# The second last image's last projection and routing, moved beside the last image's first mixture

## The chip, the cores and the metric

The kernel runs on one core of a Trainium2 chip. TensorE (PE), VectorE (DVE), ScalarE (ACT) and GpSimd (POOL) each work through their own instruction stream in order; SyncE (SP) issues the DMAs in order too. The time is device microseconds for one execution; the median of several executions is given. Beside it stands one execution taken with the hardware profiler, from which all durations come.

## The reference

Four images of 32 x 32 positions and 256 channels pass through four layers, each image on its own. A token is one position, so an image is 1024 tokens.

```python
# layer 0: convolution and a selective scan over 512 channels with 64 states
x = layernorm(src) @ w_in + b_in;  x = gelu(depthwise_conv3x3(x) + conv_b)
dt, Bm, Cm = split(x @ w_x);  dt = softplus(dt @ w_dt + dt_bias)
h = exp(dt * A) * h + (dt * x) * Bm          # for each token, in order
y = (h * Cm).sum(states) + x * D_skip
x = src + layernorm(y) @ w_out + b_out
# layer 1: grouped 3x3 bottleneck with a residual
# layer 2: masked attention with 8 heads, then a mixture of 8 experts (hidden 256), top 2
t = t + layernorm(ln(t) + attn(ln(t)));  t = t + moe2(ln(t))
# layer 3: selective scan over 512 channels with 16 states, then a mixture (hidden 512), top 2
p, gate = split(ln(t) @ W_in);  u = silu(p @ W_conv + b_conv)
B, C = split(u @ W_bc);  dt = softplus(u @ W_dt + b_dt)
h = exp(dt * A) * h + dt * B * u;  y = (h * C).sum(states) * silu(gate)
t = t + y @ W_out + b_out
t = t + moe3(ln(t))     # logits, softmax, two best experts, sum of weight * (gelu(x W1 + b1) W2 + b2)
```

## The kernel before

**The scans set the pace.** `SCANS` (line 31) lists eight scans as (layer, image), the last two being (3, 2) and (3, 3). `scans` (line 366) cuts each into units of 128 rows (channels times states) by 1024 tokens: 256 units for a layer 0 scan, 64 for a layer 3 scan, sixteen of them for each of four channel groups `d`. For unit k, `load` fetches dt, repeated over the states, into a `dA` tile (five buffers) by DMA; `decay` turns it to exp(dt * A) on ACT; `first` repeats dt * x over the states with two bf16 matmuls into `ps_rep` (two buffers, from the tile `S`); DVE multiplies this by B and runs the scan into `h`; POOL multiplies `h` by C; `pair` sums two units over the states on PE into `ps_y`, which ACT copies out and SP stores. B and C lie repeated over the partitions in the tiles `rows0` and `rows1`, two buffers each, fetched by `chunk` with `S`, `AHEAD` = 12 units ahead.

**All else is laid between the units.** Each stage of an image is a generator that issues some instructions and yields: `front` (layer 0 up to its scan), `middle` (line 1870: `back0`, `layer1`, `attention`, `moe(2)`, `front3`) and `last` (line 1880: `back3`, `moe(3)`, store of the image). `run` (line 562) steps through the scan units, adds up an estimate of each engine's time, and after each half unit calls `advance` (line 540) up to `TICKS` = 2 times while no other engine's sum is ahead of DVE's. Stages follow one another; the next is the first in `STAGES` whose scan is far enough. This is all decided when the program is built. On the chip each engine only follows its stream and its semaphores.

**Where a scan needs a stage.** A scan of layer 3 needs what `front3` writes for its image (`parts` and `dt`, for each `d`). `chunks_ahead` (line 414) looks for it 12 units ahead and puts it off while more than `LATEST` = 5 units remain. Then `need` (line 527) advances the stage until the data are written, with no scan unit between; `self.alone` tells the attention that it may use the scan's PSUM. For the last scan (3, 3), this comes five units before the end of scan (3, 2): the rest of image 3's attention, its `moe(2)` and `front3` up to its first channel group are issued there, and the last four units of scan (3, 2) are replicated, multiplied and scanned behind them.

**`back3` (line 1797)** fetches the tokens `t` kept by `front3`, and for each `d` the silu gate and y; a `Wait` holds it until that scan has stored y. POOL adds the bias row to the tokens (`add_rows`) and multiplies y by the gate (`gated`); PE projects with `W_out` into `ps_o`; DVE adds that to the tokens `tb`. **`moe` (line 1518)** fetches the first expert's weights; takes the norm (statistics on DVE, a log and an exponential on ACT, then the tokens through ACT); transposes on PE (`ps_tr`); multiplies by the router (`ps_lg`); finds the two best experts in `route` on DVE with one `Exp` on ACT; transposes the weights (`ps_ct`) and adds the experts' second bias (`ps_b`). Then it runs over 8 experts and two halves of the tokens: `one` issues the matmuls of `ps_h` and, one block later, `ps_e`; `two` issues `Gelu` on ACT and the weighted addition to `tb` on DVE. Weights have two buffers and are fetched one expert ahead. PSUM tiles of side work come from `ps` (line 180), three in rotation.

All pools of side work lie on the right side of SBUF, stacked. Where a helper records the call, the profile has line 124 for it.

Of the kernel before, what the change touches and what calls it, by code (L numbers as in the profile page):

```python
# [7 lines left out]
F32 = mybir.dt.float32  # L8
# [8 lines left out]
P = 128  # L17
NB = 4
# [23 lines left out]
AHEAD = 12  # L42
LATEST = 5


# [82 lines left out]

class Wait(tuple):
    pass  # L130


class Hybrid:
# [232 lines left out]
    def scans(self, mp, psum):  # L366
# [9 lines left out]
        for scan in SCANS:  # L376
            G = P // self.states[scan[0]]
            units += [
                (scan, d, c, i, j)
                for d in range(DC) for c in range(2) for i in range(32 // G) for j in range(2)  # L380
            ]
        chunks, rows, waiting = {}, {}, []
        state = {}
        self.scan_psum = psum
        y = None

        def chunk(k):

            if k >= len(units):
                return  # L390
            scan, d, c, i, j = units[k]
            if (c, i, j) != (0, 0, 0):
                return
            n = self.states[scan[0]]
            self.need(scan, d)
            if d == 0:
                bct = self.mem["bc", *scan]
                pair = []
                for t in range(2):
                    x = mp.tile([P, L], F32, tag=f"rows{t}", name=f"rows{t}", bufs=2)  # L400
                    nc.sync.dma_start(
                        x, bct[t * n : (t + 1) * n, :].unsqueeze(1).to_broadcast([n, P // n, L])
                    )
                    pair.append(x)
                rows[scan] = pair
            S = mp.tile([3 * 32, 4, L], BF16, tag="S", name="S", bufs=2)
            for s in range(3):
                nc.sync.dma_start(
                    S[32 * s : 32 * s + 32, :, :],
                    self.mem["parts", *scan, d][s].rearrange("(j p) t -> p j t", p=32),  # L410
                )
            chunks[scan, d] = S

        def chunks_ahead(k, late=False):

            if not late and k + AHEAD < len(units) and units[k + AHEAD][2:] == (0, 0, 0):
                waiting.append(k + AHEAD)
            while waiting:  # L420
                scan, d = units[waiting[0]][:2]
                if ("parts", *scan, d) not in self.ready:
                    if waiting[0] - k > LATEST:
                        break
                    if not late:
                        return True
                    self.alone = True
                chunk(waiting.pop(0))
                self.alone = False
            return False  # L430

        def load(k):
            if k >= len(units):
                return
            scan, d, c, i, j = units[k]
# [9 lines left out]
        def decay(k):  # L445
            if k >= len(units):
                return
            scan, d, c, i, j = units[k]
# [6 lines left out]
        def first(k):  # L455
            if k >= len(units):
                return
# [39 lines left out]
        for k in range(AHEAD):  # L497
            chunk(k)
        for k in range(4):
            load(k)  # L500
        decay(0)
        decay(1)
        first(0)
        for k in range(len(units) + 4):
            waits = chunks_ahead(k)
            load(k + 4)
            if not waits:
                first(k + 1)
            decay(k + 2)
            if k < len(units):  # L510
                a, inp = state.pop(k)
                B, Cm = rows[units[k][0]]
                nc.vector.tensor_tensor(inp, inp, B, ALU.mult)
            yield
            if k < len(units):
                h = mp.tile([P, L], F32, tag="h", name="h", bufs=5)
                nc.vector.tensor_tensor_scan(h, a, inp, 0.0, ALU.mult, ALU.add)
                nc.gpsimd.tensor_tensor(h, h, Cm, ALU.mult)
                state[k] = h
            if k % 2 == 1 and 2 <= k < len(units) + 2:  # L520
                pair(k - 2)
            if waits:
                chunks_ahead(k, True)
                first(k + 1)
            yield
# [991 lines left out]

    def moe(self, which, b, tb):

# [5 lines left out]
        KH = hidden // P  # L1525
        with tc.tile_pool(name=f"m{which}{b}", bufs=1, side="right") as op:
            xT = op.tile([P, 2, L], F32, name="xTm")
            cw = op.tile([P, TB, NEXP], F32, name="cw")

# [6 lines left out]

            weights = {0: expert_weights(0)}
            with tc.tile_pool(name=f"mg{which}{b}", bufs=1, side="right") as gp:
                xn = gp.tile([P, TB, C], F32, name="xnm")
# [51 lines left out]
                yield from self.pipe(range(TB // 2), last, add, cost=1.0)  # L1591

            hidden_of = {}
            got = {}
# [201 lines left out]

    def back3(self, b, tb):
        nc, tc = self.nc, self.tc
        with tc.tile_pool(name=f"h{b}", bufs=1, side="right") as sp:
            nc.sync.dma_start(tb, self.mem["t", b])  # L1800
# [69 lines left out]
    def middle(self, b):  # L1870

        with self.tc.tile_pool(name=f"t{b}", bufs=1, side="right") as tp:
# [3 lines left out]
            yield from self.attention(b, tb)  # L1876
            yield from self.moe(2, b, tb)
            yield from self.front3(b, tb)

    def last(self, b):  # L1880
        with self.tc.tile_pool(name=f"e{b}", bufs=1, side="right") as tp:
            tb = tp.tile([P, TB, C], F32, name="tb")
# [48 lines left out]
```

## Time and profile before

| | us |
|---|---|
| median of 3 executions | 6504.83 |
| lowest, highest | 6499.96, 6507.34 |
| profiled execution, its own time | 6499.29 |
| its span | 6497.3 |
| PE busy | 5253.9 (81%) |
| DVE busy | 5119.6 (79%) |
| ACT busy | 3415.4 (53%) |
| POOL busy | 3646.8 (56%) |

All times inside the kernel are counted from the start of the span. The page gives busy times, the span in 40 slices of 162 us, and groups of instructions as output tile<-input tiles, shapes and count. In a table of windows each row has the window, its length, busy us and number of instructions of PE, PE's weight loads, DVE, ACT and POOL, the granted PE clock as a share of full speed, the DMA engines' share and GB/s. One f32 matmul of the program appears as two records.

### The profile page before, as it was taken

To read this page: it belongs to the slowest core of one execution; us is meant where nothing else is said; L and a number is where in the kernel's file an instruction comes from. 1 tells how busy PE (TensorE), PEld (TensorE's weight loads), DVE (VectorE), ACT (ScalarE), POOL (GpSimd) and SP (SyncE) were. 2 spreads that over 40 slices of the span, in tenths; PEclk is the share of its full clock that TensorE was granted. 3 is DMA by queue.
4 is the path that set the end of the run, shared out by engine and by line. 5 is a ranking of instruction groups with operands and counts; after the bars stand their busy time and mean duration, and the time that the engine had idled before them with its cause. 6 is when DMAs were issued, how large, how long until landed. Compare 5 with 4: busy or idle time off the path is not lost. (4 is left out here: it accounts for less than half of the span.)

```text
span 6497.3 us, 59722 instructions
## 1 busy us (share of the span) xinstructions
PE 5253.9 (81%) x20235; PEld 2124.1 (33%) x20320; DVE 5119.6 (79%) x4310; ACT 3415.4 (53%) x4095; POOL 3646.8 (56%) x1793
## 2 busy tenths in 40 slices
PE   6667868689797569979689679798699688978979
PEld 2022212222342022234145232252255222524656
DVE  3978988988898998889889988898899981258311
ACT  3346656355576335567568445577387354246311
POOL 2957677765557666555856665556756661055200
PEclk9577868689898569979789789898699689878989
DMA  2454554643355566335635664345544750156221
GB/s 101 145 163 159 180 163 160 198 150 124 119 174 170 180 169 164 113 128 184 195 132 176 195 159 135 112 146 178 182 164 163 196 148 15 46 147 166 68 67 34
DMA packets 348077, 936.58 MB, mean 144 GB/s; under 512 B 37140, under 2 KB 119648, under 8 KB 346144
## 3 DMA queue, kind: packets, MB, share of 16 engines
q1 hardware_dynamic: 345616, 930.35, 46.0%
q0 software_dynamic: 2128, 2.13, 0.2%
q8 instruction: 168, 2.75, 0.2%
q14 instruction: 165, 1.35, 0.1%
HBM read 842.59 MB, written 93.95 MB: 144 GB/s over the span
## 5 line engine op out<-in xcount | busy, mean ns | idle before, releaser
L124 POOL TENSOR_TENSOR h<-h,rows 128x1024 f32<-128x1024 f32 x1280 | 3033.0, 2372 | 1835.8 <-DVE h L124 1572.9
L124 DVE TENSOR_TENSOR_SCAN h<-dA,ps_rep 128x1024 f32<-128x1024 f32 x1280 | 2923.7, 2284 | 131.4 <-ACT dA L124 3.1
L124 DVE TENSOR_TENSOR ps_rep<-ps_rep,rows 128x1024 f32<-128x1024 f32 x1280 | 1551.7, 1212 | 188.5 <-PE ps_rep L124 183.9
L124 ACT ACTIVATE dA<-dA,A_L_conv_A_log 128x1024 f32<-128x1024 f32 x1024 | 1147.7, 1144 | 612.1 <-DMA dA<-dt 547.2
L124 PE MATMUL ps_rep<-S,spread_L_conv_A_log 96*128 96x512 bf16 x2048 | 763.2, 463 | 767.6 <-DVE h L124 716.2
L124 PE MATMUL ps_y<-h,collect_L_conv_A_log 128*32 128x512 f32 x4096 | 775.8, 767 | 61.5 <-POOL h L124 61.0
L124 PE MATMUL ps_h<-xTm,we 128*128 128x512 f32 x1536 | 714.2, 604 | 0.0
L124 PE MATMUL ps_e<-we,h_m 128*128 128x256 f32 x3072 | 700.4, 380 | 2.3 <-ACT h_m L124 2.3
L124 PEld LDWEIGHTS <-spread_L_conv_A_log 96*128 96x128 bf16 x2048 | 159.9, 103 | 1568.9 <-DVE h L124 1236.1
L124 ACT ACT_TABLE_LOAD x483 | 619.7, 1283 | 59.4 <-PE ps_h L124 44.1
L124 PEld LDWEIGHTS ps_e<-we,h_m 128*128 128x128 f32 x3072 | 579.4, 190 | 152.5 <-issue 61.1
L124 DVE SCALAR_TENSOR_TENSOR tb<-ps_e,cw,tb 128x256 f32<-128x256 f32 x512 | 219.9, 474 | 409.3 <-PE ps_e L124 409.2
L124 ACT ACTIVATE h_m<-ps_h,cols 128x512 f32<-128x512 f32 x384 | 260.2, 687 | 501.4 <-PE ps_h L124 498.9
L124 ACT ACTIVATE p<-ps_sc 128x512 f32<-128x512 f32 x432 | 234.5, 594 | 386.0 <-PE ps_sc L124 255.4
L124 PEld LDWEIGHTS ps_h<-xTm,we 128*128 128x128 f32 x1536 | 291.9, 193 | 331.7 <-issue 286.9
L124 ACT ACTIVATE dA<-dA,A_L_attn_A_log 128x1024 f32<-128x1024 f32 x256 | 290.6, 1146 | 200.0 <-DMA dA<-dt 172.3
L124 PE MATMUL ps_rep<-S,spread_L_attn_A_log 96*128 96x512 bf16 x512 | 185.8, 451 | 173.8 <-DVE h L124 161.0
L124 PE MATMUL ps_at<-p,v 128*32 128x512 f32 x1024 | 277.6, 623 | 4.8 <-ACT sums L124 4.6
L124 PE MATMUL ps_at<-p,ones 128*32 128x512 f32 x1024 | 277.6, 623 | 0.0
L124 PE MATMUL ps_sc<-qT,kT 32*128 32x512 f32 x864 | 262.9, 665 | 14.2 <-ACTq L1318 8.1
L124 PE MATMUL ps_cv<-pad,diag 128*128 128x512 f32 x576 | 262.3, 597 | 0.0
L124 PEld LDWEIGHTS ps_y<-h,collect_L_conv_A_log 128*32 128x32 f32 x4096 | 99.4, 119 | 436.9 <-issue 222.6
(327 smaller groups left out, 4865.4 us busy)
## 6 DMA issues: line engine op xcount, KB each, us to landing
dA<-dt SPq DMA_DIRECT2D x1280, 512.0 KB
we<-in_L_ffn_W_dram SPq DMA_DIRECT2D x64, 512.0 KB
parts<-parts SPq DMA_DIRECT2D x64, 384.0 KB
S<-parts SPq DMA_DIRECT2D x96, 256.0 KB
dt<-sp_r SPq DMA_DIRECT2D x64, 256.0 KB
y<-yo SPq DMA_DIRECT2D x128, 128.0 KB
y_back<-y SPq DMA_DIRECT2D x64, 256.0 KB
we<-in_L_ffn_w_dram SPq DMA_DIRECT2D x64, 256.0 KB
```

Source lines behind the costliest of these rows:

```text
L124: return got(*args, **kw)
```

## The change

Five things are done.

- `DRAIN` = 4 empty entries stand in the list of units ahead of the first unit of the last scan, and that unit's data are waited for only one entry ahead (`LATEST` stays 5 for the others). So all 64 units of scan (3, 2) are issued, and their sums stored, ahead of the wait. `upto` issues `load` and `decay` for a unit only when its chunk has been fetched.
- B and C of a scan lie in one tile `rows`, with two buffers.
- `back3` and `moe` can take their pools from the left side. `moe` can yield a `Pause` between its routing and its experts; the experts' pool is then taken, and the first weights fetched, after the pause.
- For image 3, `middle` runs `moe(2)` through `beside`: after each of its steps one step of `ahead(2)` is issued, which is image 2's `back3` and `moe(3)` up to the pause. Its tokens lie in a buffer of `rows`.
- `last(2)` resumes that generator: the experts and the store. `last(3)` is as before.

```diff
@@ -41,6 +41,7 @@
 SCATTERED = 1
 AHEAD = 12
 LATEST = 5
+DRAIN = 4
 
 
 
@@ -127,6 +128,10 @@
 
 
 class Wait(tuple):
+    pass
+
+
+class Pause:
     pass
 
 
@@ -379,14 +384,20 @@
                 (scan, d, c, i, j)
                 for d in range(DC) for c in range(2) for i in range(32 // G) for j in range(2)
             ]
+        final = next(k for k, unit in enumerate(units) if unit[0] == SCANS[-1])
+        units[final:final] = [None] * DRAIN
+        final += DRAIN
         chunks, rows, waiting = {}, {}, []
-        state = {}
-        self.scan_psum = psum
+        state, ahead = {}, {"load": 0, "decay": 0}
+
+        def unit(k):
+            return units[k] if 0 <= k < len(units) else None
+        self.scan_psum, self.scan_pool = psum, mp
         y = None
 
         def chunk(k):
 
-            if k >= len(units):
+            if unit(k) is None:
                 return
             scan, d, c, i, j = units[k]
             if (c, i, j) != (0, 0, 0):
@@ -395,14 +406,13 @@
             self.need(scan, d)
             if d == 0:
                 bct = self.mem["bc", *scan]
-                pair = []
+                both = mp.tile([P, 2, L], F32, tag="rows", name="rows", bufs=2)
                 for t in range(2):
-                    x = mp.tile([P, L], F32, tag=f"rows{t}", name=f"rows{t}", bufs=2)
                     nc.sync.dma_start(
-                        x, bct[t * n : (t + 1) * n, :].unsqueeze(1).to_broadcast([n, P // n, L])
+                        both[:, t, :],
+                        bct[t * n : (t + 1) * n, :].unsqueeze(1).to_broadcast([n, P // n, L]),
                     )
-                    pair.append(x)
-                rows[scan] = pair
+                rows[scan] = both[:, 0, :], both[:, 1, :]
             S = mp.tile([3 * 32, 4, L], BF16, tag="S", name="S", bufs=2)
             for s in range(3):
                 nc.sync.dma_start(
@@ -415,12 +425,12 @@
 
 
 
-            if not late and k + AHEAD < len(units) and units[k + AHEAD][2:] == (0, 0, 0):
+            if not late and unit(k + AHEAD) and units[k + AHEAD][2:] == (0, 0, 0):
                 waiting.append(k + AHEAD)
             while waiting:
                 scan, d = units[waiting[0]][:2]
                 if ("parts", *scan, d) not in self.ready:
-                    if waiting[0] - k > LATEST:
+                    if waiting[0] - k > (1 if waiting[0] == final else LATEST):
                         break
                     if not late:
                         return True
@@ -429,9 +439,16 @@
                 self.alone = False
             return False
 
+        def upto(what, one, k):
+            while ahead[what] <= k:
+                to = unit(ahead[what])
+                if to and to[:2] not in chunks:
+                    break
+                if to:
+                    one(ahead[what])
+                ahead[what] += 1
+
         def load(k):
-            if k >= len(units):
-                return
             scan, d, c, i, j = units[k]
             n = self.states[scan[0]]
             G = P // n
@@ -443,8 +460,6 @@
             state[k] = a
 
         def decay(k):
-            if k >= len(units):
-                return
             scan, d, c, i, j = units[k]
             G = P // self.states[scan[0]]
             col = (d * P + 64 * c + 32 * j) // G + i
@@ -453,7 +468,7 @@
             )
 
         def first(k):
-            if k >= len(units):
+            if unit(k) is None:
                 return
             scan, d, c, i, j = units[k]
             spread = self.tables[scan[0]][1]
@@ -496,31 +511,31 @@
 
         for k in range(AHEAD):
             chunk(k)
-        for k in range(4):
-            load(k)
-        decay(0)
-        decay(1)
+        upto("load", load, 3)
+        upto("decay", decay, 1)
         first(0)
         for k in range(len(units) + 4):
             waits = chunks_ahead(k)
-            load(k + 4)
+            upto("load", load, k + 4)
             if not waits:
                 first(k + 1)
-            decay(k + 2)
-            if k < len(units):
+            upto("decay", decay, k + 2)
+            if unit(k):
                 a, inp = state.pop(k)
                 B, Cm = rows[units[k][0]]
                 nc.vector.tensor_tensor(inp, inp, B, ALU.mult)
             yield
-            if k < len(units):
+            if unit(k):
                 h = mp.tile([P, L], F32, tag="h", name="h", bufs=5)
                 nc.vector.tensor_tensor_scan(h, a, inp, 0.0, ALU.mult, ALU.add)
                 nc.gpsimd.tensor_tensor(h, h, Cm, ALU.mult)
                 state[k] = h
-            if k % 2 == 1 and 2 <= k < len(units) + 2:
+            if k % 2 == 1 and unit(k - 2):
                 pair(k - 2)
             if waits:
                 chunks_ahead(k, True)
+                upto("load", load, k + 4)
+                upto("decay", decay, k + 2)
                 first(k + 1)
             yield
 
@@ -1515,7 +1530,7 @@
                 self.router[which].rearrange("p k e -> p (k e)"), ps[:, : 2 * NEXP]
             )
 
-    def moe(self, which, b, tb):
+    def moe(self, which, b, tb, side="right", pause=False):
 
         nc, tc, a = self.nc, self.tc, self.a
         w1, w2, b1, hidden = (
@@ -1523,9 +1538,16 @@
             else (a["L3_ffn_W1"], a["L3_ffn_W2"], self.vec["L3_ffn_b1"], 512)
         )
         KH = hidden // P
-        with tc.tile_pool(name=f"m{which}{b}", bufs=1, side="right") as op:
-            xT = op.tile([P, 2, L], F32, name="xTm")
-            cw = op.tile([P, TB, NEXP], F32, name="cw")
+        with ExitStack() as stack:
+            xp = stack.enter_context(tc.tile_pool(name=f"mx{which}{b}", bufs=1, side=side))
+            xT = xp.tile([P, 2, L], F32, name="xTm")
+            cw = xp.tile([P, TB, NEXP], F32, name="cw")
+            weights, op = {}, None
+
+            def begin():
+                nonlocal op
+                op = stack.enter_context(tc.tile_pool(name=f"m{which}{b}", bufs=1, side=side))
+                weights[0] = expert_weights(0)
 
             def expert_weights(e):
                 we1 = op.tile([P, 2, hidden], F32, tag="we1", name="we1", bufs=2)
@@ -1534,8 +1556,9 @@
                 nc.sync.dma_start(we2, w2[e].rearrange("(k p) n -> p k n", p=P))
                 return we1, we2
 
-            weights = {0: expert_weights(0)}
-            with tc.tile_pool(name=f"mg{which}{b}", bufs=1, side="right") as gp:
+            if not pause:
+                begin()
+            with tc.tile_pool(name=f"mg{which}{b}", bufs=1, side=side) as gp:
                 xn = gp.tile([P, TB, C], F32, name="xnm")
                 yield from self.norm(gp, tb, TB, xn, "lnm")
                 yield from self.turned(xn, TB, xT)
@@ -1590,6 +1613,9 @@
 
                 yield from self.pipe(range(TB // 2), last, add, cost=1.0)
 
+            if pause:
+                yield Pause()
+                begin()
             hidden_of = {}
             got = {}
 
@@ -1794,9 +1820,9 @@
                     vec["L3_attn_b_dt"], u,
                 )
 
-    def back3(self, b, tb):
+    def back3(self, b, tb, side="right"):
         nc, tc = self.nc, self.tc
-        with tc.tile_pool(name=f"h{b}", bufs=1, side="right") as sp:
+        with tc.tile_pool(name=f"h{b}", bufs=1, side=side) as sp:
             nc.sync.dma_start(tb, self.mem["t", b])
             y = sp.tile([P, DC, L], F32, name="y_back")
             gate = sp.tile([P, DC, L], F32, name="gate_back")
@@ -1874,10 +1900,44 @@
             yield from self.back0(b, tb)
             yield from self.layer1(b, tb)
             yield from self.attention(b, tb)
-            yield from self.moe(2, b, tb)
+            moe = self.moe(2, b, tb)
+            if b == NB - 1:
+                self.other = self.ahead(b - 1)
+                moe = self.beside(moe, self.other)
+            yield from moe
             yield from self.front3(b, tb)
 
+    def beside(self, main, other):
+
+        for cost in main:
+            yield cost
+            if other is None:
+                continue
+            more = next(other)
+            assert not isinstance(more, Wait) or tuple(more) in self.done
+            if isinstance(more, Pause):
+                other = None
+            elif not isinstance(more, Wait):
+                yield more
+        while other is not None:
+            more = next(other)
+            if isinstance(more, Pause):
+                other = None
+            else:
+                yield more
+
+    def ahead(self, b):
+
+        tb = self.scan_pool.tile([P, TB, C], F32, tag="rows", name="tb_rows", bufs=2)
+        yield from self.back3(b, tb, "left")
+        yield from self.moe(3, b, tb, "left", True)
+        self.nc.sync.dma_start(self.image(self.out, b), tb)
+        yield 1.0
+
     def last(self, b):
+        if b == NB - 2:
+            yield from self.other
+            return
         with self.tc.tile_pool(name=f"e{b}", bufs=1, side="right") as tp:
             tb = tp.tile([P, TB, C], F32, name="tb")
             yield from self.back3(b, tb)
```

## The prediction

> **What bounds the kernel now.** I read the slices first, then busy time stage by stage over the last 1,130 us, then the groups of the best-filled stage, then the DMA queue at the start of the last image.
>
> The slices (a digit is a fortieth of the span, 162 us):
>
> ```profile
> PE   6667868689797569979689679798699688978979
> DVE  3978988988898998889889988898899981258311
> PEclk9577868689898569979789789898699689878989
> ```
>
> Up to slice 31 DVE, which carries the scans, is 80 to 90% busy. From slice 33 it has little to do, and PE carries the end. So a change at the end is priced in PE time and in PE's idle time. Stages of the end (PE, PEld, DVE, ACT, POOL busy us with instruction counts, granted PE clock, DMA share, GB/s):
>
> ```profile
> 5370.00:5482.00 112.00, 110.42 (x626) 28.91 (x638) 11.08 (x18) 48.17 (x56) 7.58 (x6) 1.00 0.00 1
> 5499.00:5549.00 50.00, 29.59 (x87) 19.79 (x88) 15.98 (x63) 15.28 (x28) 9.97 (x8) 0.56 0.07 22
> 5549.00:5654.00 105.00, 104.03 (x370) 69.92 (x368) 28.08 (x65) 21.21 (x30) 0.00 (x0) 1.00 0.10 30
> 5764.00:5866.00 102.00, 57.80 (x161) 13.15 (x162) 88.49 (x57) 45.41 (x54) 89.55 (x52) 0.56 0.93 239
> 5866.00:5940.00 74.00, 55.99 (x216) 28.08 (x215) 64.19 (x77) 28.51 (x37) 33.69 (x15) 0.70 0.58 146
> 5940.00:6060.00 120.00, 117.87 (x485) 62.97 (x484) 113.69 (x86) 102.47 (x100) 70.83 (x30) 1.00 0.64 158
> 6064.00:6192.00 128.00, 127.57 (x456) 86.42 (x456) 17.03 (x39) 25.84 (x37) 0.00 (x0) 1.00 0.09 27
> 6192.00:6269.00 77.00, 39.89 (x137) 30.27 (x138) 14.72 (x51) 9.37 (x18) 14.82 (x12) 0.62 0.38 116
> 6269.00:6497.00 228.00, 221.86 (x768) 146.19 (x767) 28.54 (x65) 43.98 (x64) 0.00 (x0) 0.99 0.10 33
> ```
>
> In order: image 3's attention, with no scan beside it; its first mixture's routing; that mixture's experts; (image 3's `front3`, left out, ends at 5764); the last scan, at first beside the rest of `front3` and image 2's `back3`, then beside image 2's routing, then beside image 2's experts; the rest of those experts alone; image 3's `back3` and routing; its experts. What to see: experts alone fill PE (127.57 of 128). In the first 176 us of the last scan PE works 114 us, mostly at a clock of 0.56, because the experts, the only heavy PE work left, can't begin until image 2 has been projected and routed. That is what the change takes from there.
>
> The rates come from the groups of 5940 to 6060:
>
> ```profile
> L124 DVE TENSOR_TENSOR_SCAN h<-dA,ps_rep 128x1024 f32<-128x1024 f32 x31 | 70.8, 2285 | 3.5 <-ACT dA L124 0.5
> L124 DVE TENSOR_TENSOR ps_rep<-ps_rep,rows 128x1024 f32<-128x1024 f32 x31 | 37.6, 1212 | 3.2 <-PE ps_rep L124 3.2
> L124 PE MATMUL ps_h<-xTm,we 128*128 128x512 f32 x105 | 48.7, 597 | 0.0
> L124 PE MATMUL ps_e<-we,h_m 128*128 128x256 f32 x192 | 43.7, 381 | 1.7 <-ACT h_m L124 1.7
> L124 PE MATMUL ps_rep<-S,spread_L_attn_A_log 96*128 96x512 bf16 x60 | 18.0, 381 | 0.5 <-DVE h L124 0.5
> L124 PE MATMUL ps_y<-h,collect_L_attn_A_log 128*32 128x512 f32 x128 | 17.0, 605 | 0.0
> ```
>
> 31 scan units in 120 us: 3.87 us a unit with experts beside it, PE and DVE both full. A unit's own PE work is (18.0+17.0)/31 = 1.13 us. An f32 matmul of the program is two records here, so an `ps_h` costs about 0.86 us and a `ps_e` 0.43 us at full clock.
>
> **The change, part by part.** The instruction streams of both kernels are the same up to image 3's attention, but for the two rows tiles becoming one, so nothing is expected before 5,350 us. I follow one point, the issue of the last scan's row loads (5761.8 in the trace), and then the end.
>
> *Drain.* Four units of scan (3,2) that came after `front3` now run beside the attention, which is bound by PE (110.42 of 112 us). 4 x 1.13 = +4.5 us there. The three empty ticks issue nothing.
>
> *Moved into the first mixture.* 16 DMA loads (`tb_rows`, gate, y, `w_out`) go on SP right behind the first expert's two weight loads, at 5499, where DMA is 7% busy; behind them stand the second expert's weights, wanted only at about 5560. In the tail the same loads take 6197 to about 6218, so here they should have landed by 5522. POOL gets 4 + 8 operations of 1.26 us; four of moe 2's own adds stand among them and end near 5525, before DVE needs them at 5535. PE gets its share not in the gap of 5499 to 5549 but behind it: in PE's order the 32 `ps_o` alternate with the first `ps_h`, and the transposes, logits and bias matmuls lie among the experts. So it is paid in full on a full PE. Here a rule bears. In the trace these matmuls at a clock of 0.5 to 0.7 take 5.5 (`ps_tr`), 6.84 (`ps_lg`), 1.87 (`ps_ct`), 7.19 (`ps_b`) and 15.7 to 18.6 us (`ps_o`), some 38 us. The Trainium skill (TensorE: Matmul & The Clock Gate, What's actually happening) says that the clock doubles after about 3.4 us of activity and falls back after an idle window of that length. By the rows 38 us; by the rule, with a busy PE, half for the first four and 64 x 0.216 = 13.8 for `ps_o`: 10.7 + 13.8 = 24.5 us. I take 24.5, as the expert stage shows a clock of 1.00; the other is the upper bound.
>
> *Stalls of that mixing.* PE, DVE and ACT each now serve two chains in order. Behind a late transpose wait the next expert's matmuls; behind an `Exp` of the routing waits a `Gelu`, and for that PE. ACT gets four table loads in this stage. A load is 1.28 us in the trace and the next activation starts within 0.02 us; the Trainium skill (ScalarE: Activation LUTs, What ACT_TABLE_LOAD costs) counts a further 1.38 us of drain per switch. By the row 5 us on ACT, by the rule 10.6; I take the row. Three rotating PSUM tiles give about two 1.72 us steps of slack, so part of this hides. Between 0 (all hidden) and 20 us (every load and every hand-over shown), I take 5. The point thus moves by 4.5 + 24.5 + 5 = +34, to 5796.
>
> *The last scan.* Its pipeline was filled behind the four old units; now it starts empty. Two row loads, S and the first dA are 2.3 MB; at the 200 to 250 GB/s of that time and an `Exp` behind it the first scan comes some 14.5 us after the point (10 to 18). In PE's order the first expert matmul now stands behind unit 12 of 64 (before: 37 of 68). The first 12 units at 3.6 us, as between 5815 and 5860: 43. The other 52 at 3.87: 201; PE's own sum there, 90 `ps_h` + 160 `ps_e` + 52 units, is 77 + 69 + 59 = 205, so nearly balanced. The first expert's weights are issued just ahead of use, where before they came some 50 us early: 3 us (0 to 6), with the replication for the scan queued behind them. The last unit's multiply and sum: 4. Together 265.5, so the scan ends at 6061.5; before, 6063.9.
>
> *Experts left over.* Behind the last `ps_y` stood 68 `ps_h` and 160 `ps_e` (128 us); now 38 and 96. By the row of 6064 to 6192, 128 x (30x0.86 + 64x0.43)/(68x0.86 + 160x0.43) = 53 us fewer: about 75. They end at 6136.5 instead of 6191.6.
>
> *The last image.* It keeps its 305 us, less one wait:
>
> ```profile
> 6192.51 0.38 SPq L1885 DMA_DIRECT2D out_dram<-tb  x1
> 6197.02 0.34 SPq L1800 DMA_DIRECT2D tb<-t  x1
> ```
>
> The load of `tb` waits 4.5 us for the store, as both images used one place; now the other image lies in the rows buffer. -4.5.
>
> Sum: -55 - 4.5, about -60 us on a span of 6497.3 (6499.3 with what lies around it). The median shown is 6504.8, 5.5 above the profiled execution; I carry the difference over: 6445.
>
> **Rivals.**
> 1. *The mixing isn't hidden at all*: the moved chain adds what it takes alone, the 77 us of the stage at 6192, instead of 24.5 + 5. Then -60 + 47 = -13 to -20 us, some 6488. For it: strict order on three engines and small dependent steps. Against: its steps are spread over some 70 expert steps, DVE is 27% and ACT 20% busy there.
> 2. *The last scan with experts from the start is held by DMA*, as in the row at 5764 (share 0.93, 239 GB/s) where ACT waited for dA. Then 4.5 us a unit over 52 units: +33, so 6478. Against: in that row image 2's 5.5 MB came as well, and they are gone; at 5940 to 6060 the share was 0.64.
> 3. *Slower.* Expert weights come late. They stand on SP behind dA loads that wait for a free buffer, PE waits for them in order, and the scan's `ps_rep` waits behind. Nearly six experts now fall into the scan. At w us lost for each it costs 6w: above 10 us the gain is gone, at 13 us the time is about 6522. For it: the loads are issued in the order of use, with two buffers. Against: from 5940 on the same order left PE 118 of 120 us busy.
>
> **How the numbers follow.** The first account 66%, rival 1 13%, rival 2 11%, rival 3 10%. A measurement can tell about 0.2%, 13 us, from no change. Own range of the likeliest: stalls 0 to 20, cold matmuls up to +13, fill -4 to +4, pace 3.7 to 4.1 (-9 to +12), weights -3 to +3; not all at one end, so 6424 to 6470. To keep no more than 2 in 10 out, rivals 1 and 2 are taken in: 6422 to 6488. Faster 0.87 (all of the first two accounts and most of rival 1), same 0.04, slower 0.09.
>
> **What would show it.** The row loads of the last scan issued near 5796; the experts of moe 2 about 30 us longer at a clock near 1; the first scan of the last image 14 us after its row loads; 3.9 us a unit with PE and DVE both above 90% from unit 12 on; some 75 us of experts after the scan; `tb<-t` issued right behind the store. Wrong if the expert stage grows by far more than 30 us, if the clock there falls, or if PE waits for `we` in the scan.

## The result, and the profile after

The changed kernel takes 6463.75 us (median of 5, 6452.28 to 6474.96) against 6504.34 (median of 5, 6495.26 to 6507.34) for the kernel before in the same session: a ratio of 0.9938, 95% interval 0.9926 to 0.995, 40.6 us less. Forecast was 6445 with a range of 6422 to 6488: the sign and the mechanism hold, about a third of the expected gain is missing. The profiled execution is the slowest of the five: 6474.96 us, span 6473.2.

Its slices, below, counted from 0: only the end differs by more than a digit. In 33 DVE has 3 in place of 1: the drained units run there, and the slice begins 20 us earlier in the span than in the profile of before, while older units still run. In 34 it has 3 in place of 2, for it now carries image 2's routing beside image 3's first mixture. In 35 it has 1 in place of 5 and in 37 6 in place of 3, for the last scan lies later.

```profile
PE   6667868689797568979789779898699689787979
DVE  3978988988898998889889998798989983318611
```

Busy time in the stages of the end (window, length, then busy us and count of PE, weight loads, DVE, ACT, POOL, granted clock, DMA share, GB/s), in the order of the rows of before: attention with the four drained units; routing of the first mixture; its experts with the moved chain; (the rest of `front3` up to the last scan left out); the first 12 units of the last scan; its start with experts; the balanced part; left-over experts; image 3's projection and routing; its experts.

```profile
5380.00:5496.00 116.00, 116.00 (x668) 30.41 (x660) 21.27 (x24) 51.14 (x63) 16.79 (x10) 1.00 0.01 3
5513.00:5563.00 50.00, 23.64 (x78) 18.20 (x79) 22.20 (x63) 13.21 (x25) 24.75 (x20) 0.54 0.56 137
5563.00:5700.00 137.00, 136.47 (x513) 93.14 (x513) 41.32 (x111) 35.97 (x54) 0.00 (x0) 0.98 0.08 24
...
5810.00:5886.00 76.00, 31.07 (x77) 8.82 (x78) 49.99 (x33) 33.20 (x42) 49.63 (x29) 0.59 0.84 211
5886.00:5950.00 64.00, 62.75 (x253) 32.98 (x252) 57.78 (x42) 61.22 (x60) 35.45 (x15) 1.00 0.71 175
5950.00:6087.00 137.00, 134.52 (x557) 71.55 (x559) 132.57 (x101) 113.82 (x109) 84.68 (x36) 1.00 0.64 165
6093.00:6168.00 75.00, 73.95 (x268) 50.54 (x266) 10.51 (x24) 15.27 (x22) 0.00 (x0) 1.00 0.06 18
6168.00:6245.00 77.00, 41.02 (x137) 31.04 (x138) 14.49 (x49) 9.37 (x18) 14.81 (x12) 0.60 0.38 116
6245.00:6473.00 228.00, 221.80 (x768) 145.98 (x766) 28.26 (x65) 43.98 (x64) 0.00 (x0) 0.99 0.10 33
```

The moved work is inside 137 us that PE fills (136.47) at a clock of 0.98. The left-over experts fell from 128 to 75 us. The last scan with experts beside it is now full on PE and DVE at once. Two rows have not improved: the first 12 units (PE 31 of 76 us), and the 77 us between the two images' experts, as long as before.

This execution was already late before the change touches anything: unit 300 of the scans starts at 1442.7, in the profile of before at 1431.7, and the 60th unit of scan (3, 2), the last one that both kernels issue ahead of the drain, at 5373.8 against 5363.7. The instruction streams up to there differ in nothing but the rows tile. I take 10.1 us off below; the first experiment asks whether that is allowed. The ledger of the prediction, then, in us:

| step | predicted | measured |
|---|---|---|
| row loads of the last scan issued | 5796 | 5807.8 - 10.1 = 5797.7 |
| from there to the first scan | 14.5 | 16.2 |
| first scan to the scan of unit 12 | 43 + 3 = 46 | 65.4 |
| from there to the start of the last unit's scan, 51 units | 51 x 3.87 = 197.4 | 197.4 |
| from there to the left-over experts | 7.6 | 6.2 |
| left-over experts | 75 | 75 |
| end of these to the end of the span | 305 - 4.5 = 300.5 | 305.2 |

Two steps are wrong: 19.4 us in the third row, 4.7 in the last. With the small ones (1.7 + 1.7 - 1.4) they make 26.1 us. The forecast's rows end at 6437.0, 60.3 before the 6497.3 of before, and -60.3 + 26.1 = -34.2; the spans say the same, 6473.2 - 10.1 - 6497.3 = -34.2.

DVE's own timeline shows the third row (start, duration, operation, and in brackets its wait and for whom):

```profile
5824.02 2.29 DVE L125 TENSOR_TENSOR_SCAN h<-dA,ps_rep 128x1024 f32<-128x1024 f32 x1 [0.94 <-ACT dA L125]
5828.90 1.50 DVE L125 TENSOR_TENSOR sp_x<-sp_l,parts 128x512 f32<-128x512 f32 x1 [2.59 <-ACT parts L125]
5830.32 0.68 DVE L125 SCALAR_TENSOR_TENSOR sp_e<-ps_dt,sp_e 128x512 f32<-128x512 f32 x1
...
5850.98 1.14 DVE L125 TENSOR_TENSOR sp_x<-sp_l,parts 128x512 f32<-128x512 f32 x1 [2.73 <-ACT parts L125]
...
5875.32 2.29 DVE L125 TENSOR_TENSOR_SCAN h<-dA,ps_rep 128x1024 f32<-128x1024 f32 x1
5888.04 1.23 DVE L125 TENSOR_TENSOR ps_rep<-ps_rep,rows 128x1024 f32<-128x1024 f32 x1 [10.42 <-PE ps_rep L125]
5889.40 2.29 DVE L125 TENSOR_TENSOR_SCAN h<-dA,ps_rep 128x1024 f32<-128x1024 f32 x1
```

Units 0 to 11 take (5875.32 - 5824.02) / 11 = 4.66 us each: between the scans stand the `sp_x` and `sp_e` (tiles of the softplus) of `front3`'s remaining channel groups, two of them with a wait for ACT. Then, ahead of unit 12, DVE waits 10.4 us for the replication on PE. The waits of PE in 5800 to 5920 (total, times, longest) name what PE waits for:

```profile
PE ps_rep L125 <- DVE h L125: 24.1, 8, 6.9
PE ps_rep L125 <- DMA S<-parts: 18.7, 1, 18.7
PE ps_h L125 <- DMA we<-in_L_ffn_W_dram: 10.0, 1, 10.0
```

The second line is the pipeline filling. The third is the first matmul of image 2's experts, waiting for weights; the scan's replication stands behind it in PE's order. SP's queue at that place, and at the store of image 2:

```profile
5871.86 0.55 SPq L665 DMA_DIRECT2D parts<-parts  x1
5877.56 0.38 SPq L1554 DMA_DIRECT2D we<-in_L_ffn_W_dram  x1
...
6167.89 0.38 SPq L1934 DMA_DIRECT2D out_dram<-tb_rows  x1
6168.33 0.57 SPq L1826 DMA_DIRECT2D tb<-t  x1
```

The load of `tb` does come right behind the store, as forecast. It just wins nothing.

### The profile page after: what moved, and what is told of

The parts are those of the page before. It is cut to its first block, busy times and chain, and to the rows that moved or that the text cites. A ratio compares the mean times of both kernels' runs of the same rounds, so it can differ in the third digit from the quotient of the medians.

```text
span 6473.2 us, 59804 instructions
## 1 busy us (share of the span) xinstructions
PE 5239.5 (81%) x20320; PEld 2119.7 (33%) x20320; DVE 5129.3 (79%) x4310; ACT 3452.5 (53%) x4128; POOL 3646.4 (56%) x1793
## 5 line engine op out<-in xcount | busy, mean ns | idle before, releaser
L125 DVE SCALAR_TENSOR_TENSOR tb<-ps_e,cw,tb 128x256 f32<-128x256 f32 x448 | 191.9, 473 | 274.6 <-PE ps_e L125 274.5
```

The lines of the kernel that those rows point to most:

```text
L125: return got(*args, **kw)
```

## The experiments

In each, "the kernel before" ran in the same session on the same chip; its medians were 6505.46, 6508.0 and 6507.29 in the three sessions (experiments 1 to 4, 5 to 8, 9 to 11). The changed kernel itself ran in the session of the result (6463.75) and as experiment 8 (6469.29); where it is compared with a kernel of another session, the stretches of the traces are given beside the medians.

**1. Is the early delay the change's? The rows tile alone.** Kernel before, with B and C in one tile:

```diff
-                    x = mp.tile([P, L], F32, tag=f"rows{t}", name=f"rows{t}", bufs=2)
...
+                both = mp.tile([P, 2, L], F32, tag="rows", name="rows", bufs=2)
```

> The kernel before with one edit, B and C in one tile. In the profile after, the scans of the first 1500 us ran 10 us late although no instruction there is in another place. Theory: that is scatter between executions; the median stays at 6504 within 7 us and the first units of this profile are not all 10 us late at the same places (units 32 to 64, 224 to 320). Rival: the merged tile costs it; then some 6514 and the same 10 us at the same places.

Measured: 6505.76, ratio 1.0002 (0.9996 to 1.0009). The tile costs nothing. Among the profiles with the same early stream, unit 300 starts at 1445.0 here, 1448.2 in the changed kernel taken again, and 1431.3 with the early weights of experiment 4. So the 10 us are scatter between executions, and subtracting them is fair.

**2. The drain alone.** The changed kernel with image 2's part put back where it was: `moe(2)` without `beside`, `last(2)` as before.

```diff
             moe = self.moe(2, b, tb)
-            if b == NB - 1:
-                self.other = self.ahead(b - 1)
-                moe = self.beside(moe, self.other)
             yield from moe
...
-        if b == NB - 2:
-            yield from self.other
-            return
```

> The changed kernel without the mixing: the drain, the empty entries and the merged tile stay, image 2's projection and routing are again in the stage of the last scan. Theory: the drain alone gains nothing. It puts 4.5 us on the attention, empties the scan's pipeline (16 us of filling) and leaves 25 instead of 31 units for the experts behind the routing, 16 us more of experts left at the end; against that the scan has four units fewer. About +10, so 6514. Rival: part of the gain is the drain's, the scan being shorter; then 6490 or less.

Measured: 6515.38, ratio 1.0017 (1.0008 to 1.0026). By itself the drain costs 10 us. From the first to the twelfth scan of the last image it takes (5839.4 - 5787.5) / 11 = 4.72 us a unit; in the kernel before and with the rows tile alone, neither of them drained, 3.89. So the slow start belongs to the drain and not to the moved work: without old units to fill the time after the row loads, the first new ones run while `front3` still works on its other channel groups (four `sp_x` fall among them, in the kernel before two). The waits of DVE in the first twelve units, first with the drain alone (5787 to 5840), then in the kernel before (5788 to 5832):

```profile
DVE sp_x L125 <- ACT parts L125: 6.5, 2, 3.7
DVE sp_x L124 <- ACT parts L124: 0.6, 1, 0.6
```

The waits make 5.9 of the 9.1 us between 11 x 4.72 and 11 x 3.89; the two further `sp_x` with their `sp_e` are about the rest.

**3. The moved chain in one piece.** All of it is issued after the first step of `moe(2)`, ahead of the rest:

```diff
-        for cost in main:
-            yield cost
-            if other is None:
-                continue
+        done = object()
+        first = next(main, done)
+        assert first is not done
+        yield first
+        while other is not None:
             more = next(other)
...
+        yield from main
```

> The changed kernel, but image 2's projection and routing are issued in one piece ahead of image 3's first mixture instead of step by step beside it. Theory: what counts is that PE has other work under the moved chain. In one piece it costs its 77 us as at the end of the kernel, where it cost 34 beside the mixture; about +43, so 6507, no gain left over the kernel before. Rival: engines that work in order have most of it one after the other anyhow; then 6464 to 6480.

Measured: 6510.02, ratio 1.0011 (1.0005 to 1.0018): the whole gain is gone, the median is 46 us above that of the changed kernel. PE's waits in 5500 to 5620:

```profile
PE ps_o L125 <- POOL y_back L125: 29.7, 4, 19.5
PE ps_tr L125 <- ACT xnm L125: 14.4, 2, 7.6
PE ps_ct L125 <- DVE cw L125: 11.6, 2, 6.3
```

That is 56 us of waiting for POOL, ACT and DVE, of which 43 (29.7, 7.6 and 5.3) stand in image 2's chain and the rest in image 3's own routing behind it. The chain lies from 5502 to 5585, and PE is busy for 40 of these 83 us. From the first weight load of `moe(2)` to its last `ps_e` it takes 229.1 us, against 187.8 with the steps interleaved and 154.1 in the kernel before: 75 us more than before, near the 77 that the chain takes alone at the end of the kernel. So moving it is worth nothing where it still runs alone; laying each step between experts is what pays. This is rival 1, built as a kernel: in this stage it costs 41 us more than the interleaved steps, by the medians 46; the prediction gave it 47.

**4. The first expert's weights early.** Image 2's first weights go into a pool of their own during image 3's `front3`:

```diff
             if pause:
                 yield Pause()
+                wp = stack.enter_context(tc.tile_pool(name=f"mw{which}{b}", bufs=1, side=side))
+                we1 = wp.tile([P, 2, hidden], F32, name="we1_first")
+                nc.sync.dma_start(we1, w1[0].rearrange("(k p) n -> p k n", p=P))
+                we2 = wp.tile([P, KH, C], F32, name="we2_first")
+                nc.sync.dma_start(we2, w2[0].rearrange("(k p) n -> p k n", p=P))
+                weights[0] = we1, we2
+                yield Pause()
...
```

and in `front3` of image 3, ahead of `conv`: `assert isinstance(next(self.other), Pause)`.

> The changed kernel, but the weights of the first expert of image 2's second mixture are fetched during front3 of image 3 into a place of their own, about 100 us ahead of use. In the profile after, PE waits 10.0 us for them at unit 12 of the last scan, and DVE 10.4 us for the replication queued behind. Theory: that wait is on the path, so about -10, 6454, and no idle PE before the first ps_h there. Rival: the scan then meets the next limit (dA loads, the rest of front3) and less than 4 us come back.

Measured: 6450.81 (6443.93 to 6465.7), ratio 0.9927 (0.9914 to 0.9941). PE's waits in the same window as above no longer have the line for `we`:

```profile
PE ps_rep L125 <- DVE h L125: 23.5, 8, 6.2
PE ps_rep L125 <- DMA S<-parts: 17.9, 1, 17.9
PE ps_h L125 <- ACT h_m L125: 3.2, 2, 2.0
```

The first 12 units still take 4.68 us each: the two causes of the third row are separate. Unit 12 follows with 0.7 us of delay instead of 10.5. Not all of that is won: the 51 units after it now take 201.4 us instead of 197.4, in which DVE waits 6.9 us for the replication on PE, in the changed kernel 2.4 from unit 13 on. From the start of scan (3, 3) to the end of the span it takes 643.5 us, in the changed kernel 649.2 and, taken again, 649.6. So the traces give the early weights 6 us; the medians give 13 and the two ratios, whose intervals overlap, 7.

**5 and 6. The same trick once more.** On top of experiment 4, image 3's own `back3` and routing run in steps beside image 2's last experts, with two of its steps for each expert step (5) or one (6). `beside` takes the number of steps and passes over a step whose `Wait` isn't met; `rest` issues what is left up to the pause:

```diff
+    def ahead_last(self, b):
+        with self.tc.tile_pool(name=f"e{b}", bufs=1, side="right") as tp:
+            tb = tp.tile([P, TB, C], F32, name="tb")
+            yield from self.back3(b, tb)
+            yield from self.moe(3, b, tb, "right", True, True)
+            self.nc.sync.dma_start(self.image(self.out, b), tb)
+            yield 1.0
...
-            yield from self.other
+            self.next = self.ahead_last(NB - 1)
+            st = {"gen": self.next, "stop": False, "wait": None}
+            yield from self.beside(self.other, st, 2)
+            yield from self.rest(st)
```

> The kernel after, with the weights of image 2's first expert fetched early (as in the run before this one), and the same trick once more: image 3's own output projection and routing issued in small steps beside image 2's last experts, two steps for each expert step. In the kernel after that part takes 77 us alone (from the last ps_e of image 2 to the first ps_h of image 3) with PE busy 41 of it at a clock of 0.60. Theory (what pays is the spreading of small dependent steps over a full PE): 6451 - 77 + 30 (24.5 of PE work at full clock, 5 of hand-overs) = about 6404, and the trace shows no gap of PE over 5 us between the two images. Rival 1 (the stage of 75 us is too short for as many steps; each hand-over shows): 6430 or more, PE busy well below 90% in the stage of the left-over experts. Rival 2 (nothing is hidden): 6451.

> The same, but one step of image 3's projection and routing for each expert step of image 2; the experts end first and about ten steps are left to run alone. Theory: what is left alone costs its own latency, some 10 to 20 us more than with two steps to one, so about 6414 to 6424, the gap of PE seen behind image 2's last ps_e. Rival (hand-overs set the time, and two to one stalls PE more often): equal to it or faster.

Measured: 6413.69 (ratio 0.9855, 0.9839 to 0.9871) and 6422.34 (0.9869, 0.9854 to 0.9885). PE's timeline of the first shows the steps lying between the experts with waits of about a microsecond:

```profile
6109.74 2.97 PE L125 MATMUL ps_o<-w_L_attn_W_out,y_back 128*128 128x256 f32 x13
...
6138.34 0.60 PE L125 MATMUL ps_tr<-ident,xnm 128*128 128x128 f32 x4
6138.78 4.66 PE L125 MATMUL ps_lg<-wr,xTm 128*128 128x8 f32 x32
6143.28 6.02 PE L125 MATMUL ps_e<-we,h_m 128*128 128x256 f32 x16
```

PE's longest wait there is 1.3 us. From the start of the last unit's scan to the end of the span it takes 340.7 us, with the early weights alone 386.4: 45.7 less, of 47 expected. The medians give 37 less and the two ratios 47; the 6404 forecast was missed by 10 us, within the scatter just seen. With one step to one, 348.0, 7 us more, a little below the 10 to 20 expected: of the steps left alone at the end, PE waits 5.3 us for the routing's result and then 4.2 for the weights.

**7 and 8. The store behind the loads.** The ledger's last row: a wait went and nothing was won. My reading was that the loads share the DMA engines with the store, so that the wait only changed its place. In the changed kernel, only the place of image 2's store is changed:

```diff
-        self.nc.sync.dma_start(self.image(self.out, b), tb)
+        self.late = self.image(self.out, b), tb
...
             yield from self.back3(b, tb)
+            if b == NB - 1:
+                self.nc.sync.dma_start(*self.late)
             yield from self.moe(3, b, tb)
```

> The kernel after, with one edit: the store of image 2's result is issued behind image 3's loads and projection, not ahead of them. In the kernel after the store (tb) and the loads for image 3 (t, gate, y, w_out) are issued within half a microsecond and the first expert weights of image 3 come 42 us behind the store's issue, as in the kernel before, where the load of tb waited 4.5 us for the store. Theory (the loads share the DMA engines with the store, so the 4.5 us was given back): the stretch from the last ps_e of image 2 to the first ps_h of image 3 falls from 77 to about 72.5 us and the total by some 4 us against the kernel after of this call. Rival (the stage is set by its chain of PE, DVE and ACT steps, not by the arrival of its loads): 77 us and no difference.

> The kernel after once more, unchanged, so that the other runs of this call are compared with it on one chip. Theory: 6464 with 10 us of scatter to both sides, a ratio to the kernel before of 0.994. In its trace the wait of PE for the first expert weights inside the last scan is again 9 to 11 us, the first 12 units of that scan again take about 4.5 us each and the stretch between the two images' experts 77 us; if the first 1,500 us again run 10 us behind the kernel before, the rows tile costs time after all, if they do not, it was scatter.

Measured: 6441.17 (6434.93 to 6449.76) against 6469.29 (6459.19 to 6472.07) for the unchanged one. 28 us from one line, seven times what my theory gave it and not the nothing of the rival: both fell. PE's waits between the two images' experts in the changed kernel, from its first profile (6160 to 6250):

```profile
PE ps_o L125 <- POOL y_back L125: 23.5, 4, 15.3
PE ps_tr L125 <- ACT xnm L125: 7.5, 1, 7.5
PE ps_ct L125 <- DVE cw L125: 5.9, 1, 5.9
```

With the late store, SP's queue and PE's timeline:

```profile
6113.43 0.37 SPq L1556 DMA_DIRECT2D we<-in_L_ffn_W_dram  x1
6113.86 0.50 SPq L1826 DMA_DIRECT2D tb<-t  x1
...
6162.57 0.40 SPq L1945 DMA_DIRECT2D out_dram<-tb_rows  x1
```

```profile
6147.65 13.98 PE L125 MATMUL ps_e<-we,h_m 128*128 128x256 f32 x64
6161.46 13.98 PE L125 MATMUL ps_o<-w_L_attn_W_out,y_back 128*128 128x256 f32 x64
6182.99 5.62 PE L125 MATMUL ps_tr<-ident,xnm 128*128 128x128 f32 x16 [7.55 <-ACT xnm L125]
```

and SP's queue in the unchanged kernel's second profile:

```profile
6115.36 0.37 SPq L1556 DMA_DIRECT2D we<-in_L_ffn_W_dram  x1
6164.50 0.38 SPq L1934 DMA_DIRECT2D out_dram<-tb_rows  x1
6164.93 0.57 SPq L1826 DMA_DIRECT2D tb<-t  x1
```

What the loads share with the store is SP's order. The store can only go when the last expert has been added; SP issues nothing from the last weight load to it, 49 us long, and image 3's tokens, gates and y, which need nothing of that image, stand behind. Let past, they start at 6113.86, POOL has multiplied y while PE runs experts, and the 23.5 us of `ps_o` waiting for `y_back` are gone: the projection follows the last expert without a gap. It also takes 14.0 us itself, where it took 18.6 in pieces with waits between: PE comes from the experts, and the granted clock is 1.00 there (6161 to 6175). From the start of the last unit's scan to the end: 357.3 us instead of 386.9.

The changed kernel taken again also settles two lines: its wait for `we` is 9.6 us and its first 12 units take 4.70.

**9, 10 and 11. Does it add up, and does it need the change?** Experiment 9 is 4 and 7 together, no interleaving of image 3. Experiment 11 is experiment 5 again. Experiment 10 is the kernel before with the rows tile, places of their own for image 3's loads, and the late store:

```diff
...
     def last(self, b):
+        if b == NB - 1:
+            tb = self.scan_pool.tile([P, TB, C], F32, tag="rows", name="tb_rows", bufs=2)
+            yield from self.back3(b, tb, "left")
+            self.nc.sync.dma_start(*self.late)
+            yield from self.moe(3, b, tb)
...
+            if b == NB - 2:
+                self.late = self.image(self.out, b), tb
+                return
             self.nc.sync.dma_start(self.image(self.out, b), tb)
```

> The kernel after with two small edits of earlier runs together: the weights of image 2's first expert fetched early, and the store of image 2's result issued behind image 3's loads and projection; nothing of image 3 is interleaved with image 2's experts. Theory (the store stood at the head of SP's queue waiting for the last expert, and image 3's loads behind it; this cost 28 us, apart from the 13 us of the late weights): 6467 - 13 - 28 = about 6426. What then is left for the interleaving of both images (6413.7) is some 12 us: the waits of PE for the normalized rows (7.5 us), the routing (5.9 us) and the cold clock. Rival (the two edits share one cause, or the interleaving's 37 us over the early weights alone is mostly its small steps): 6440 or more.

> The kernel before, not drained and nothing moved, with the late store alone: image 3's t goes into a tile of the rows buffer and its y, gate and w_out into space on the left, so that none of these loads needs the place of image 2's data, and the store of image 2's result is issued behind them. Theory (SP's order alone held image 3's projection back, in the kernel before too): the stretch from the last ps_e of image 2 to the first ps_h of image 3 falls from 77 to about 48 us and the time to 6507 - 28 = about 6479, ratio 0.9957. Rival (the gain of the late store needs the changed kernel, because there the left-over experts and the loads overlap otherwise): no difference, 6507, or about 6502 if only the 4.5 us of waiting for the store goes.

> The kernel with both images' projection and routing interleaved (and the early weights) once more, for comparison with the two others on one chip: 6414 with 8 us to both sides, about 12 us below the kernel with the early weights and the late store only.

Measured: 6428.98 (ratio 0.988, 0.9861 to 0.9898), 6476.01 (0.9955, 0.9939 to 0.997) and 6411.51 (0.9857, 0.9839 to 0.9875). The two causes add: experiment 9 lies 38 us below the 6467 of the changed kernel (the mean of its two medians), 13 + 28 expected. In the traces, from the start of scan (3, 3) to the end, it is 613.6 us against 649.4, 36 less, where the late store alone wins 28.5 (620.9) and the early weights 6. The kernel before wins 31 us with the late store, three quarters of what the whole change brings. PE's waits for `y_back` between the two images' experts in the kernel before (6185 to 6275), and its timeline with the late store, where none is left:

```profile
PE ps_o L124 <- POOL y_back L124: 24.5, 4, 16.6
...
6183.02 13.98 PE L124 MATMUL ps_e<-we,h_m 128*128 128x256 f32 x64
6196.83 13.98 PE L124 MATMUL ps_o<-w_L_attn_W_out,y_back 128*128 128x256 f32 x64
6218.36 5.62 PE L124 MATMUL ps_tr<-ident,xnm 128*128 128x128 f32 x16 [7.55 <-ACT xnm L124]
```

In this kernel two things were freed together, SP's order and the place of the loads; which of them would have held without the other isn't told here. In experiment 7 only the order changed. Interleaving both images is the fastest version, 17.5 us below experiment 9 in the same session (12 expected).

## Why the prediction was right, and where it was off

*Drain and moved work: right.* The stage of the first mixture grew by 33.7 us (29.5 predicted), the attention by 3.9 (4.5). Of the 33.7, 6.4 are further waits of PE (5 predicted) and 27.3 the moved matmuls, for which the durations of the rows said 38 us and the clock rule of the Trainium skill (TensorE: Matmul & The Clock Gate, What's actually happening) 24.5. The trace is much nearer to the rule; how much activity it takes to raise the clock, no run here shows. In the group view of 5563 to 5700 (busy us, mean ns):

```profile
L125 PE MATMUL ps_o<-w_L_attn_W_out,y_back 128*128 128x256 f32 x59 | 14.7, 404 | 0.0
L125 PE MATMUL ps_b<-b,cT 8*128 8x256 f32 x16 | 4.5, 400 | 0.0
L125 PE MATMUL ps_lg<-wr,xTm 128*128 128x8 f32 x32 | 3.6, 253 | 0.0
```

`ps_lg` is 3.6 us where alone it takes 6.8, `ps_b` 4.5 where it takes 7.2. With `ps_tr` (2.4) and `ps_ct` (1.2) these four take 11.7 us, against 21.4 in the rows, where the granted clock was 0.5 to 0.7, and 10.7 by the rule; here it was 0.98. What is left of the 27.3 us, 15.6, is the projection, priced at 13.8; its first six records still lie in the stage with the clock of 0.54.

*Stalls of the mixing: right in size, wrong in place.* PE lost only 0.5 us between the experts. The time went into the routing of the first mixture itself, where PE now waits 17.2 us for the normalized rows and 9.9 for the routing's result; before, 14.9 and 6.3, so 5.9 more. Why these two waits grew was not tested.

*"The first 12 units at 3.6 us, as between 5815 and 5860: 43": wrong by 12.* I took the rate from a stage in which `front3` was nearly over. The drained scan's first units run beside its softplus work, at 4.66. The start of the row of 5764 to 5866, where both overlap, would have been the better place, but it gives only half of the difference: from 5772.2 on, twelve units take 4.12 us each there. The other half comes with the drain, as experiment 2 shows.

*"The first expert's weights ... 3 us (0 to 6)": wrong by 7.* The wait is 10 us. I named it as a sign of being wrong and priced it too low: I counted from the load's issue, but SP issues it 5.7 us after the DMA ahead of it. SP's own waits (5865 to 5892; total, times, longest) name what it waits for:

```profile
SPq L1554 <- DMA parts<-parts: 5.0, 2, 4.8
```

That is `front3`'s store of `parts`, ahead of the load in the queue: the weights' pool is taken only after `front3`, and its first load waits until that store has landed. It is the same in experiments 3, 7 and 8 (4.1, 4.4 and 4.0 us at the longest), and gone in experiment 4, where the weights have a place of their own. The wait went with it; of its cost the trace gives 6 us back, as told there. Rival 3 was this mechanism at six experts' times; it happened once only, as PE's waits for `we` over the whole span (10.0 us) show; from the second expert on the loads are issued a block ahead.

*"-4.5": wrong, and the row was misread.* I quoted two lines of SP's queue, the store and the load 4.5 us behind it, and took the gap between them for the price. The price stood ahead of both lines: the store itself waited for the last expert, and everything behind it on SP with it. Removing the small wait left the large one. SP's own waits in the kernel before (6150 to 6200) show both, the store's and the load's:

```profile
SPq L1885 <- DVE tb L124: 48.7, 1, 48.7
SPq L1800 <- DMA out_dram<-tb: 4.1, 1, 4.1
```

In the changed kernel the first is still there, 48.7 us, and the second is gone. It could also have been seen by asking, for the first `ps_o`, who released it (POOL), for POOL who (the loads), and for the loads what stood ahead in SP's order. Experiments 7 and 10 show 28 and 31 us.

*The balanced part and the left-over experts: right.* 3.87 us a unit, 75 us left. Rival 2, the scan held by DMA, did not come: the share is 0.64 in 5950 to 6087.

*The range.* 6464 lies even in the narrower range of the first account, 6424 to 6470, but not because each term kept its own: the weights had -3 to +3 and came 7 over, the rate of the first 12 units and the end of the kernel had no range at all. The terms that were given most room, stalls (0 to 20) and cold matmuls (up to 13 more), came in at 6.4 and 2.8 more, and what they left of the range took up the others.

## What to carry to other kernels

Small dependent steps cost their latency wherever they stand alone and little more than their PE time between the matmuls of a full stage; moving such a chain without interleaving it gained nothing here (6510 against 6464). In a queue that issues in order, a store of a result is a wait for the whole computation before it: put the loads of the next piece ahead of it, and give them a place of their own. When a start is moved earlier, take its rate from a stage with the same neighbours, not from the steady part. And ask for the waits of the queue itself: SP's waits name the 48.7 us of the store, and the store that held the first weights, where PE's waits name only POOL and the weights.

## What was not expected

Executions of one kernel differ by some 10 us already in the first quarter of the span, with the same instructions: unit 300 started between 1431.3 and 1448.2 us. A difference of a profile's absolute times below that says nothing; differences inside a stage repeat better (the wait for `we` was 10.0, 9.6 and 10.1 us in three profiles, the stretch from the last unit's scan to the end 386.4, 386.9 and 386.4; but from the start of scan (3, 3) to the end 708.3 in the kernel before and 712.3 with the rows tile alone). An edit of one line, the place of a store in SP's queue, gave more than half of what the large change gave.
